# A transformer-like block on one core: the first phase's transfers in program order on one queue

## The chip, the cores and the metric

The kernel runs on one core of a Trainium2 chip. The time is device microseconds of that core for one execution; 2199.59 us is the median of three (2198.95 to 2201.4). One further execution was recorded by the hardware profiler. It took 2197.51 us, and its span, from the first instruction to the last, is 2195.7 us. Engines are named as in the profile: PE multiplies, PEld loads its weights, DVE, ACT and POOL work elementwise, and SP only issues transfers. SPq is SP's queue: it issues in order, and a transfer whose data or target is not ready holds up all that stand behind it.

## The reference

`x` is 8 sequences ("batches" below) of 1024 rows with 512 features. Both branches start from the same layer norm, and their product is added to `x`:

```python
def _L0_attn_ref(x, Wq, Wk, Wv, Wo, Wg, decay_logits, out_scale):
    q = x @ Wq
    gate = softmax(x @ Wg, axis=-1)
    for i in range(3):
        k = x @ Wk[i]
        v = x @ Wv[i]
        w = sigmoid(decay_logits[i]) ** expn * causal     # a later row only
        retrieved = (q @ k.T * w) @ v
        blended = blended + gate[..., i:i + 1] * retrieved
    return blended @ Wo * out_scale

def _L0_ffn_ref(x, lut, gate_idx, up_idx, down_idx):
    h = silu(x @ lut[gate_idx].T) * (x @ lut[up_idx].T)
    return h @ lut[down_idx].T

xn = layernorm(x)
out = x + attn(xn) * silu(ffn(xn))
```

The FFN's weights are given as indices into a table of 16 words, so they have to be looked up before they can be multiplied.

## The kernel before

The program has two phases. **Phase 1** (`phase_1`, up to about 627 us) normalizes and transposes `x`, does the attention, and builds the FFN's weights; it leaves its results in DRAM. **Phase 2** does the FFN and the output. Only phase 1 and the border between the two are touched here.

Phase 1 runs a loop over `b` from 0 to 8, each with eight steps `k`. In loop `b` three generators advance by turns, and so does the building of the weights:

- `project(b)`, called `newer`: for row tile `c = 7 - k` it transposes `x` on PE into PSUM (`pt`), and ACT copies that to `xnT` (L329). Then come `values` (`pv`, then `v`), `features` (`pq`, then `qT` and `kT`) and half a `softmax`, which makes the gates `g` on DVE. The gates go to DRAM as `gTd` (L355) and return, broadcast over the partitions, as `ga` (L359).
- `project(b-1)`, called `ending`: the rest of the previous batch. In steps 0 to 3 DVE makes the sums `ts` (L417) for phase 2, and PE the other half of the features. At the end of the generator, three transfers write `xnT` (L424, L425) and `ts` (L426) to DRAM as `xsd`. In the program this end is reached only when loop `b` has run all its steps.
- `chunks(b-1)`, called `older`: the attention itself, with `pk`, `psc`, `pu` and `po` on PE, `pr` (L468) and `ga` times `qT` (L441) on DVE. ACT copies `po` into `bl` (L489), and after the eighth chunk the whole `bl` is written as `bld` (L503).
- `weights`: for each tile, index loads (`idx`), a tree of table look-ups on DVE (L176 to L200), sums on POOL, and the writes `wgud`, `quadd` and `wdd`. `build_some` advances it by single yields, spread between the other steps.

Buffers that matter: `xnT` has two, so batch `b` writes where batch `b-2` lay. `ts` has one. `x` tiles have four, `idx` and `wgu` two each.

PE, DVE, ACT and POOL keep the order in which the program was traced; `keep_order` links each instruction to the one before it on its engine. SP has that only for its first instructions: `keep_order(tc, seen, (mybir.EngineType.SP,))` is called in `phase_1` ahead of the loop. After these, the framework's scheduler places the transfers on SP's queue.

In the order that it made, the two `xsd<-xnT` of a batch stand in the loop that fills `xnT`, or just behind it, and `xsd<-ts` in the middle of the next loop, where the sums are done; all three come before the `bld` of that next loop.

At the border phase 2 starts with `load_x(0)` (L599), which reads `xsd` of batch 0 into `xs`. Its place in SBUF overlaps buffers of phase 1, so it waits for the last batch's `xsd` writes too. `zs` (L878) are matmuls that keep PE running meanwhile, and `fs` (L631) is the first that needs `xs`.

Of the kernel before, what the change touches and what calls it, by code (L numbers as in the profile page):

```python
# [2 lines left out]

# [7 lines left out]
F32 = mybir.dt.float32  # L11
# [27 lines left out]
def recurrent_block(ctx: ExitStack, tc, x, wq, wk, wv, wo, wg, decay_logits, out_scale, lut, gidx, uidx, didx, out):  # L39
# [51 lines left out]
    def more_weights(wvg_sb, wqk_sb):  # L91
        nc.scalar.dma_start(out=wvg_sb[:, :, NI * D :], in_=wg.rearrange("(c p) d -> p c d", p=P))
        for i in range(NI):
            nc.scalar.dma_start(
                out=wvg_sb[:, :, i * D : (i + 1) * D], in_=wv[i].rearrange("(c p) d -> p c d", p=P)
            )
        yield
        nc.sync.dma_start(out=wqk_sb[:, :, :D], in_=wq.rearrange("(c p) d -> p c d", p=P))
        for i in range(NI):
            nc.sync.dma_start(  # L100
                out=wqk_sb[:, :, (i + 1) * D : (i + 2) * D], in_=wk[i].rearrange("(c p) d -> p c d", p=P)
            )
        nc.sync.dma_start(out=wo_sb, in_=wo)


    seen = {i.name for i in nc.cur_bb.bb.instructions}
# [95 lines left out]

        yield from tree(dst, 3, 0)

    def gate_up_weights(build, pool, pair_pool):

        for o, (s, m) in enumerate(OCH):  # L210
            n = 2 * NV * m
            idx = build.tile([P, NB], I32, name="idx", tag="idx", bufs=2)
            iv = idx[:, :n].rearrange("p (a b) -> p a b", b=m)
            gs, us = (src[:, s : s + m].rearrange("(c p) b -> p c b", p=P) for src in (gidx, uidx))
            nc.sync.dma_start(out=iv[:, 2:6, :], in_=gs)
            nc.sync.dma_start(out=iv[:, 0:2, :], in_=us[:, 0:2, :])
            nc.sync.dma_start(out=iv[:, 6:8, :], in_=us[:, 2:4, :])
            wf = pool.tile([P, 2 * NB], F32, name="wgu", tag="wgu", bufs=2)
            yield from look_up(build, wf[:, :n], idx[:, :n], P, n)
            w = wf[:, : 2 * n].rearrange("p (k two m) -> p k two m", two=2, m=m)  # L220
            a21, a11, a12, a22, s1, s2, s3, s4 = (w[:, k] for k in range(8))
            nc.gpsimd.tensor_tensor(s1, a21, a22, ALU.add)
            nc.gpsimd.tensor_tensor(s2, s1, a11, ALU.subtract)
            yield
            nc.gpsimd.tensor_tensor(s3, a11, a21, ALU.subtract)
            nc.gpsimd.tensor_tensor(s4, a12, s2, ALU.subtract)
            nc.sync.dma_start(out=wgu_d[o], in_=wf[:, 2 * m : 2 * n].rearrange("p (a b) -> p a b", b=m))
            if o < 4 * NQ:
                if o % 2 == 0:
                    upper = w[:, 1:]  # L230
                    continue
                lower = w[:, 1:]
                to = quad_d[o // 4][:, :, o // 2 % 2, :].rearrange("p k (t m) -> p k t m", m=P)
                pair = pair_pool.tile([P, 7, 4, P], F32, name="pair", tag="pair")
                nc.sync.dma_start(out=to[:, :, 0:2, :], in_=upper)
                nc.sync.dma_start(out=to[:, :, 2, :], in_=lower[:, :, 1, :])
                b21, b22, b11, b12 = lower[:, :, 0], lower[:, :, 1], upper[:, :, 0], upper[:, :, 1]
                nc.gpsimd.tensor_tensor(pair[:, :, 0], b21, b22, ALU.add)
                yield
                nc.gpsimd.tensor_tensor(pair[:, :, 1], pair[:, :, 0], b11, ALU.subtract)  # L240
                yield
                nc.gpsimd.tensor_tensor(pair[:, :, 2], b11, b21, ALU.subtract)
                yield
                nc.gpsimd.tensor_tensor(pair[:, :, 3], b12, pair[:, :, 1], ALU.subtract)
                nc.sync.dma_start(out=to[:, :, 3:7, :], in_=pair)
                for _ in range(3):
                    yield

    def down_weights(build, pool):

        s, m = OCH[-1]
        idx = build.tile([P, NB], I32, name="idx", tag="idx", bufs=2)
        nc.sync.dma_start(out=idx[:m, :V], in_=didx[s : s + m, :])
        wf = pool.tile([P, 2 * NB], F32, name="wgu", tag="wgu", bufs=2)
        yield from look_up(build, wf[:m, :V], idx[:m, :V], m, V)
        nc.sync.dma_start(out=wdt_d, in_=wf[:m, :V])
        for j in range(NK):
            idx = build.tile([P, NB], I32, name="idx", tag="idx", bufs=2)
            for a in range(2):
                nc.sync.dma_start(out=idx[:, ts(a, V)], in_=didx[ts(j + a * NK, P), :])  # L260
            t = pool.tile([P, 2 * NB], F32, name="wgu", tag="wgu", bufs=2)
            yield from look_up(build, t[:, : 2 * V], idx, P, 2 * V)
            b11, b12, b21, b22, t1, t2, t4 = (t[:, ts(k, V // 2)] for k in range(7))
            nc.gpsimd.tensor_tensor(t1, b12, b11, ALU.subtract)
            nc.gpsimd.tensor_tensor(t2, b22, t1, ALU.subtract)
            yield
            nc.gpsimd.tensor_tensor(b12, b22, b12, ALU.subtract)
            nc.gpsimd.tensor_tensor(t4, b21, t2, ALU.subtract)
            nc.sync.dma_start(out=wd_d[j], in_=t[:, : 7 * V // 2])


    def warm_up(n):
# [5 lines left out]
    def project(b, pools, sides, kept):  # L278
# [52 lines left out]
        def values(c):  # L331

            pv = p_a.tile([P, NI * D + NI], F32, name=f"pv{b}_{c}", tag="a")
            for v in range(NV):
                nc.tensor.matmul(  # L335
                    pv, lhsT=xnT[:, v, ts(c, P)], rhs=wvg_sb[:, v, :], start=(v == 0), stop=(v == NV - 1)
                )
            nc.scalar.copy(v_sb[:, c, :], pv)

        def softmax(hf):  # L340

            n = NC // NHALF
            logits = gt[:, ts(hf, n), :]
            g = small.tile([P, n, NI], F32, name=f"g{b}_{hf}", tag="g")
            red = small.tile([P, n, 1], F32, name=f"red{b}_{hf}", tag="red")
            nc.vector.tensor_reduce(red, logits, AX.X, ALU.max)
            nc.vector.tensor_tensor(g, logits, red.to_broadcast([P, n, NI]), ALU.subtract)
            nc.scalar.activation(g, g, AF.Exp)
            yield
            sm = small.tile([P, n, 1], F32, name=f"sm{b}_{hf}", tag="sm")  # L350
            nc.vector.tensor_reduce(sm, g, AX.X, ALU.add)
            nc.vector.reciprocal(sm, sm)
            nc.vector.tensor_tensor(g, g, sm.to_broadcast([P, n, NI]), ALU.mult)
            with nc.allow_non_contiguous_dma(reason="1536 words"):
                nc.sync.dma_start(  # L355
                    out=gT_d[b][ts(hf, n * NI), :].rearrange("k p -> p k"), in_=g.rearrange("p c i -> p (c i)")
                )
            gates.append(att.tile([P, n * NI, P], F32, name=f"ga{b}_{hf}", tag="ga"))
            nc.sync.dma_start(out=gates[-1], in_=gT_d[b][ts(hf, n * NI), :].partition_broadcast(P))  # L359

        def features(hf, j):

# [25 lines left out]
        for k in range(NC):  # L388
# [9 lines left out]
                warm_up(5)  # L398
            yield
            if k >= NC // 2:  # L400
                features(1, k - NC // 2)
            half = softmax(1) if k == NC // 2 + lag else iter(())
            next(half, None)
            yield
            next(half, None)
            if k >= lag:
                values(c + lag)
            if lag and k == NC - 1:
                values(0)
            yield  # L410
        ts_ = tp.tile([P, 4, 2, U], F32, name=f"ts{b}", tag="ts")
        b11, b12, b21, b22 = (xnT[:, 2 * r : 2 * r + 2, ts(hf, U)] for r in (0, 1) for hf in (0, 1))
# [10 lines left out]
            yield  # L423
        nc.sync.dma_start(out=xs_d[b][:, 0:4, :], in_=xnT[:, :, :U])  # L424
        nc.sync.dma_start(out=xs_d[b][:, 4:6, :], in_=b22)  # L425
        nc.sync.dma_start(out=xs_d[b][:, 6:14, :], in_=ts_.rearrange("p a b u -> p (a b) u"))  # L426

    def chunks(b, pools, kept):

# [75 lines left out]
    def phase_1():  # L505
        nonlocal small, p_a, p_c, p_r
        with (
# [13 lines left out]
            tc.tile_pool(name="small", bufs=3) as small,  # L521
        ):
            pools = (xp, xnp, tp, att)
            weights = chain(gate_up_weights(build, wgup, pairp), down_weights(build, wgup))
            wvg_sb = wts.tile([P, NV, NI * D + NI], F32, name="wvg_sb", tag="wvg_sb")
            wqk_sb = wts.tile([P, NV, (NI + 1) * D], F32, name="wqk_sb", tag="wqk_sb")

# [11 lines left out]
            next(more)  # L539
            next(newer)  # L540
            next(setup)
            next(more, None)
            keep_order(tc, seen, (mybir.EngineType.SP,))
            for b in range(B + 1):
                following = project(b + 1, pools, (wvg_sb, wqk_sb), kept) if b + 1 < B else iter(())
                older = chunks(b - 1, (chk, blp), kept) if b else iter(())
                for k in range(NC):
                    next(older, None)
                    next(newer, None)
                    next(setup, None)  # L550
                    busy = (b > 0 or k >= NC // 2) and b < B
                    build_some(1 + (0 < b < B))
                    if k < NC // 2:
                        for _ in range(2):
                            next(ending, None)
# [5 lines left out]
                        next(ending, None)  # L561
                    if k >= NC - 2:
                        next(following, None)
                    next(newer, None)
                    next(older, None)
                for g in (older, ending):
# [2 lines left out]
                ending, newer = newer, following  # L569
            for _ in weights:  # L570
                pass

# [385 lines left out]
```

## Time and profile before

| | before |
|---|---|
| median of three runs | 2199.59 us |
| the profiled execution | 2197.51 us |
| its span | 2195.7 us |
| PE busy | 2171.0 us (99%) |
| DVE busy | 1111.9 us (51%) |
| PE's waits that the profile names, all together | 19.1 us |
| granted clock over the span | 0.998 |
| loop 2 / 3 / 4 to 7 / 8 of phase 1 | 75.0 / 74.6 / 74.2 each / 37.1 us |
| first `fs` of phase 2 starts | 627.53 us |

Loops are counted by `b` and measured between their ends: `bld` was issued at 139.55, 215.36, 289.57, 363.79, 438.00, 512.21, 586.42 and 623.54 us. The profile page gives shares of engines first, then the chain of work that ended last, then groups of instructions. The answers of the trace used here are lists of waits by engine (total, times, longest) and timelines (start, length, engine, line, operation; in brackets the idle time before it and what ended it).

### The profile page before, as it was taken

The numbers are of one execution on the slowest core, as the hardware profiler recorded it, in microseconds if no ns is written. First come the engines' busy times: TensorE is split into PE (matmuls) and PEld (weight loads), VectorE is DVE, ScalarE is ACT, GpSimd is POOL, SyncE is SP. The second block draws the span as 40 slices with busy tenths as digits, with TensorE's granted clock in tenths as the row PEclk, the third lists the DMA queues.
The fourth block names the chain that finished last, engine by engine and source line by source line (L and its number), as shares of the span: only waits on it lengthen the run. The fifth ranks groups of instructions, "written<-read, shape, count | busy, mean of one in ns | idle before, by whom it ended". The sixth has DMA issues, their size and how long they took to land.

```text
span 2195.7 us, 25271 instructions
## 1 busy us (share of the span) xinstructions
PE 2171.0 (99%) x9234; PEld 1599.3 (73%) x9234; DVE 1111.9 (51%) x1589; ACT 830.0 (38%) x1795; POOL 912.6 (42%) x800
## 2 busy tenths in 40 slices
PE   8989999999999999999999999999999999999998
PEld 5656666666668778678858876885787678578867
DVE  5866868688635534433533443353344335433533
ACT  3556666666434214312421441243144124313410
POOL 2525454334243454424525441543445153434512
PEclk9999999999999999999999999999999999999999
DMA  5766655534284424334432442343244234234501
GB/s 140 203 160 212 162 163 181 181 125 170 83 327 151 149 99 154 114 115 139 161 122 82 153 130 106 132 155 105 105 154 147 106 116 151 89 132 147 164 24 53
DMA packets 137153, 305.29 MB, mean 139 GB/s; under 512 B 50147, under 2 KB 71910, under 8 KB 136006
## 3 DMA queue, kind: packets, MB, share of 16 engines
q1 hardware_dynamic: 127190, 279.03, 39.1%
q0 software_dynamic: 7728, 23.86, 3.0%
q8 instruction: 73, 1.20, 0.2%
q10 hardware_dynamic: 2112, 0.79, 0.1%
q14 instruction: 50, 0.41, 0.1%
HBM read 225.72 MB, written 77.93 MB: 138 GB/s over the span
## 4 chain that ended last, share of the span: by engine, by line
PE 94%; DMA 3%; DVE 1%; POOL 1%; issue 1%; ACT 1%; ACTq 0%; SPq 0%; POOLq 0%; DVEq 0%
PE s L677 27%; PE ds L821 22%; PE fs L631 9%; PE pq L368 8%; PE pv L335 6%; PE sE L677 4%; PE fsE L631 4%; PE po L488 3%; PE ds L832 2%; PE ps L843 2%; PE psc L466 2%; PE pu L474 1%; PE pt L328 1%; DMA x<-in_x 1%; PE pk L457 1%; DMA xs<-xsd 1%
## 5 line engine op out<-in xcount | busy, mean ns | idle before, releaser
L677 PE MATMUL s<-xs,wq 128*128 128x256 f32 x2688 | 602.9, 380 | 0.0
L677 PEld LDWEIGHTS s<-xs,wq 128*128 128x128 f32 x2688 | 508.7, 190 | 78.4 <-DVE sE L704 2.7
L821 PE MATMUL ds<-wd,s 128*128 128x256 f32 x1280 | 286.7, 379 | 0.0
L821 PEld LDWEIGHTS ds<-wd,s 128*128 128x128 f32 x1280 | 243.2, 190 | 33.0
L368 PE MATMUL pq<-xnT,wqk_sb 128*128 128x512 f32 x512 | 230.3, 592 | 0.0
L821 PE MATMUL ds<-wd,h 128*128 128x256 f32 x960 | 222.9, 379 | 0.0
L821 PEld LDWEIGHTS ds<-wd,h 128*128 128x128 f32 x960 | 182.3, 190 | 52.5 <-issue 27.0
L631 PE MATMUL fs<-xs,wr 128*128 128x512 f32 (+1 forms) x480 | 215.4, 592 | 0.3 <-DMA xs<-xsd 0.3
L733 POOL TENSOR_TENSOR u<-u,e 128x512 f32<-128x512 f32 x64 | 79.9, 1270 | 276.0 <-DVE u L729 276.0
L335 PE MATMUL pv<-wvg_sb,xnT 128*128 128x387 f32 x512 | 179.6, 493 | 7.4 <-ACT xnT L329 7.4
L700 DVE TENSOR_TENSOR s<-s,e 128x512 f32<-128x512 f32 x112 | 78.4, 700 | 187.6 <-ACT s L699 187.6
L631 PEld LDWEIGHTS fs<-xs,wr 128*128 128x128 f32 (+1 forms) x480 | 86.8, 181 | 116.1 <-issue 112.4
L368 PEld LDWEIGHTS pq<-xnT,wqk_sb 128*128 128x128 f32 x512 | 92.3, 190 | 91.8 <-issue 91.8
L846 POOL TENSOR_TENSOR gx<-gx 128x512 f32<-128x512 f32 x63 | 80.3, 1275 | 184.6 <-DVE gx L844 141.1
L335 PEld LDWEIGHTS pv<-wvg_sb,xnT 128*128 128x128 f32 x512 | 93.8, 193 | 63.2 <-ACT xnT L329 7.6
L314 POOL TENSOR_SCALAR rstd<-rstd 128x1 f32<-128x1 f32 x56 | 26.9, 481 | 258.8 <-ACT junk L313 258.2
L615 POOL TENSOR_TENSOR xs<-xs 128x1792 f32<-128x1792 f32 (+1 forms) x38 | 127.9, 3382 | 7.6 <-issue 6.6
L704 DVE TENSOR_TENSOR sE<-s,e 128x512 f32<-128x512 f32 x112 | 78.3, 699 | 85.9 <-PE s L677 85.9
L862 ACT ACTIVATE gx<-ds 128x256 f32<-128x256 f32 x32 | 12.3, 384 | 287.1 <-PE ds L832 287.1
L677 PE MATMUL sE<-xs,wq 128*128 128x256 f32 x448 | 115.0, 379 | 0.0
L695 ACT COPY e<-sE 128x512 f32<-128x512 f32 x112 | 65.6, 586 | 123.7 <-PE sE L677 123.7
L737 POOL TENSOR_TENSOR h<-h,e 128x512 f32<-128x512 f32 x64 | 80.0, 1273 | 57.4 <-issue 46.4
(146 smaller groups left out, 3248.6 us busy)
## 6 DMA issues: line engine op xcount, KB each, us to landing
wq<-quadd SPq DMA_DIRECT2D x112, 896.0 KB, 4.5
xs<-xsd SPq DMA_DIRECT2D x8, 3584.0 KB, 12.1
x<-in_x SPq DMA_DIRECT2D x64, 256.0 KB, 5.2
xsd<-ts SPq DMA_DIRECT2D x8, 2048.0 KB, 7.8
gx<-in_x SPq DMA_DIRECT2D x64, 256.0 KB, 2.9
out<-gx POOLq DMA_DIRECT2D x63, 256.0 KB, 2.3
wr<-wgud SPq DMA_DIRECT2D x16, 896.0 KB, 4.6
ga<-gTd SPq DMA_DIRECT2D x16, 768.0 KB, 5.1
```

Of the source, the lines that this page charges most:

```text
L335: nc.tensor.matmul(pv, lhsT=xnT[:, v, ts(c, P)], rhs=wvg_sb[:, v, :], start=(v == 0), stop=(v == NV - 1))
L368: nc.tensor.matmul(pq, lhsT=wqk_sb[:, v, ts(j, D)], rhs=xnT[:, v, ts(hf, U)], start=(v == 0), stop=(v == NV - 1))
L488: nc.tensor.matmul(po, lhsT=lh, rhs=rh, start=(n == 0), stop=(n == len(prods) - 1))
L615: nc.gpsimd.tensor_tensor(o, x1, x2, ALU.subtract)
L631: nc.tensor.matmul(ps, lhsT=w[:, 2 * W_OF[k] + n, :m], rhs=xs[:, X_OF[k], 2 * n : 2 * n + 2, :], start=start and n == 0, stop=stop and n == 1,
L677: nc.tensor.matmul(self.t[n][:, ts(a, H)], lhsT=self.w[:, a, (0, 1, 6, 2, 3, 4, 5)[i - 1], :], rhs=self.xs[:, X_OF[self.k], D_OF[i], :], s ...
L700: nc.vector.tensor_tensor(self.t[1], self.t[1], self.e, ALU.add)
L704: nc.vector.tensor_tensor(self.t[3], self.t[2], self.e, ALU.add)
L733: nc.gpsimd.tensor_tensor(o[:, n], o[:, n], other[:, n], ALU.add)
L737: nc.gpsimd.tensor_tensor(of_h(half, n), of_h(half, n), two(other[:, n]), ALU.mult)
L821: nc.tensor.matmul(ps, lhsT=lhs[k][:, n, :], rhs=wd_sb[n][:, ts(D_OF[k], H)], start=start and n == 0, stop=stop and n == NK - 1, skip_grou ...
L846: (nc.vector if end else nc.gpsimd).tensor_tensor(g, g, xr, ALU.add)
```

## The change

Every transfer of phase 1 now keeps the place on SP's queue in which the program was traced: `keep_order` for SP is called at the end of `phase_1` and not ahead of the loop. To let a transfer stand later than the line that makes its data, `defer(n, issue)` hands it to a list, and `tick()`, called three times a step, issues what has counted down to zero. Four more edits go with that:

- index loads are issued one tile ahead of the tile that is being looked up, and the first comes one build step later;
- in batch 0, where the values lag one step behind, a second tile of values is done at `k = 4`, and the lag ends there; so the softmax comes at `k = 4` and not at `k = 5`;
- loads of `wqk` and `wo` go into the loop's first steps;
- `gTd` is written 2 ticks after its data, and `ga` read 6 ticks after them; `wgud`, `quadd`, `wdd` and `xsd<-ts` are deferred by 2 to 4 ticks.

The two other `xsd` transfers stay at the end of the generator, where the program had them.

```diff
+    later = []
+    def defer(parts, issue):
+        later.append([parts, issue])
+    def tick():
+        for entry in later:
+            entry[0] -= 1
+        for entry in [e for e in later if e[0] <= 0]:
+            later.remove(entry)
+            entry[1]()
...
-            nc.sync.dma_start(out=wgu_d[o], in_=wf[:, 2 * m : 2 * n].rearrange("p (a b) -> p a b", b=m))
+            wide = wf[:, 2 * m : 2 * n].rearrange("p (a b) -> p a b", b=m)
+            defer(3, lambda: nc.sync.dma_start(out=wgu_d[o], in_=wide))
...
+        jobs = [gate_up(o) for o in range(NO)] + [down_tail()] + [down(j) for j in range(NK)]
+        next(jobs[0])
+        yield
+        for job, following in zip(jobs, jobs[1:] + [iter(())]):
+            next(following, None)
+            yield from job
...
-            nc.sync.dma_start(out=gates[-1], in_=gT_d[b][ts(hf, n * NI), :].partition_broadcast(P))
+            ga = gates[-1]
+            defer(2, write)
+            defer(6, lambda: nc.sync.dma_start(out=ga, in_=there.partition_broadcast(P)))
...
             if k >= NC // 2:
+                if lag and k == NC // 2:
+                    values(c + 1)
+                    lag = 0
                 features(1, k - NC // 2)
-            half = softmax(1) if k == NC // 2 + lag else iter(())
+            half = softmax(1) if k == NC // 2 else iter(())
...
         nc.sync.dma_start(out=xs_d[b][:, 0:4, :], in_=xnT[:, :, :U])
         nc.sync.dma_start(out=xs_d[b][:, 4:6, :], in_=b22)
-        nc.sync.dma_start(out=xs_d[b][:, 6:14, :], in_=ts_.rearrange("p a b u -> p (a b) u"))
+        defer(2, lambda: nc.sync.dma_start(out=xs_d[b][:, 6:14, :], in_=ts_.rearrange("p a b u -> p (a b) u")))
...
-            next(more, None)
-            keep_order(tc, seen, (mybir.EngineType.SP,))
             for b in range(B + 1):
...
                 for k in range(NC):
+                    tick()
                     next(older, None)
...
-                    build_some(1 + (0 < b < B))
+                    build_some((b, k) > (0, 0) and 1 + (0 < b < B))
+                    next(more, None)
+                    tick()
...
                     if k >= NC - 2:
                         next(following, None)
+                    tick()
...
             for _ in weights:
                 pass
+            while later:
+                tick()
+            keep_order(tc, seen, (mybir.EngineType.SP,))
```

On PE, ACT and POOL the built kernel has the same instructions as before, with small moves: in batch 0 the values and features change places for four steps, and a few of POOL's sums stand a place later. On DVE the build steps stand two places later. On SP's queue most transfers have moved.

## The prediction

> **What bounds the kernel now.** I read the page's first part, PE's list of waits, and then timelines at the places that this change touches.
>
> ```profile
> PE 2171.0 (99%) x9234; PEld 1599.3 (73%) x9234; DVE 1111.9 (51%) x1589; ACT 830.0 (38%) x1795; POOL 912.6 (42%) x800
> ...
> PE pv L335 <- ACT xnT L329: 7.4, 1, 7.4
> PE pt L328 <- DVE x L320: 4.8, 4, 2.1
> PE psc L466 <- DVE ga L441: 2.8, 1, 2.8
> ```
>
> PE is the bound, so a transfer order can gain only what PE waits: 19.1 us in all. The clock adds a little. In the windows around the longest wait the granted clock is 0.50 from about 121.5 to 128 us, and the `pv` group of eight matmuls at 123.67 took 5.05 us, where it takes 2.77 elsewhere: one long wait costs another 2.3 us. What the change can lose has no such ceiling, so I looked at what each loop of phase 1 needs when it begins. Loop 3 begins at 215.0:
>
> ```profile
> 214.84 1.22 DVE L417 TENSOR_TENSOR ts<-xnT 128x1024 f32<-128x1024 f32 x1
> 215.06 0.27 ACT L489 COPY bl<-po 128x128 f32<-128x128 f32 x1 [0.85 <-PE po L488]
> ...
> 215.36 0.32 SPq L503 DMA_DIRECT2D bld<-bl  x1
> ...
> 216.16 0.60 ACT L329 COPY xnT<-pt 128x512 f32<-128x512 f32 x1
> ...
> 219.73 2.77 PE L335 MATMUL pv<-wvg_sb,xnT 128*128 128x387 f32 x8
> 219.93 0.56 DVE L468 TENSOR_TENSOR pr<-psc,w_tab 128x384 f32<-128x384 f32 x1 [1.22 <-PE psc L466]
> ...
> 223.01 0.83 PE L488 MATMUL po<-pr,v 128*128 128x128 f32 x6
> ```
>
> See there: DVE overwrites `ts` 0.2 us before the loop begins, ACT overwrites `xnT` 1.2 us after, and both go ahead at once, because both buffers were written out long before. Nothing is idle on PE. `pr` stands behind `ts` on DVE, and `po` at 223.0 needs `pr`.
>
> **The change, part by part.**
>
> *Where `xsd` stands now.* I compared the order of SP's queue in the two built kernels. In the changed one each loop's end reads: `bld`, `xsd<-xnT` (1024 KB), `xsd<-xnT` (512 KB), then, by loop, an `x` tile (256 KB), index loads (512 KB) or a weight tile (896 KB), then `xsd<-ts` (2048 KB). All of these belong to batch b-1, and they stand behind `bld`, which waits for `bl`, the last thing that the loop makes. The built order also shows the waits on the receiving side: the first `xnT` copy of batches 2 to 7 waits for both `xsd<-xnT`, and the first `ts` of batches 1 to 7 for `xsd<-ts`. In loop 3 that is DVE at 214.84 waiting for a transfer that can be issued only after 215.36.
>
> SP's list of waits already has `SPq L503 <- ACT bl L489: 32.6, 8, 7.2`, so SP stands before `bld` today too, with nothing urgent behind it. [...]
>
> *How long the burst takes.* The nearest row is a burst of the same transfers, 896+2048+256+512 = 3712 KB:
>
> ```profile
> 542.11 0.33 SPq L269 DMA_DIRECT2D wdd<-wgu  x1
> 542.53 0.38 SPq L426 DMA_DIRECT2D xsd<-ts  x1
> 543.01 0.85 SPq L297 DMA_DIRECT2D x<-in_x  x1
> 543.96 1.20 SPq L425 DMA_DIRECT2D xsd<-xnT  x1
> ...
> xsd<-ts SPq DMA_DIRECT2D x1, 2048.0 KB, 10.3
> ...
> xsd<-xnT SPq DMA_DIRECT2D x1, 512.0 KB, 10.7
> ```
>
> The last of it landed at 543.96+10.7 = 554.66, 12.55 us after the first issue: 3.38 us per 1000 KB. [...] From `bld` to `xsd<-ts` the new bursts are 4864 KB (loop 2), 5248 (loops 3, 4, 5 and 7), 4352 (loop 6) and 4096 (loop 8): 16.4, 17.7, 14.7 and 13.8 us by the row.
>
> *What PE loses.* After the landing DVE does `ts` 1.22, two short softmax steps 0.33, two build steps 1.6, `ga` 0.55 and `pr` 0.56: 4.3 us. `po` was due 8.0 us after the loop's begin, and `bld` is issued 0.36 after it. So PE waits 0.36 + burst + 4.3 - 8.0 = burst - 3.3: 13.1 in loop 2, 14.4 in each of loops 3, 4, 5 and 7, 11.4 in loop 6; together 82.1. In loop 8 `po` is due 5.25 us after the begin, `bld` goes at 0.5, and there are no build steps (2.65 us of DVE): 11.7. Sum **93.8 us** [...]. The wait for `xnT` lies inside: `bld` and the two writes are 2048 KB, 6.9 us, so `pv` slips by about 3 us, and then `po` waits for the rest. Behind the waiting `ts` stand all of DVE's build steps; nobody else needs them sooner. Behind the waiting `xnT` on ACT stand the next tile's normalization and the copies of `pq` and `pv`, all ready before 225.
>
> *The clock.* Seven waits of over 7 us. By the row each costs 2.3: **16.1 us**. [...]
>
> *After the wait* DVE needs 9.1 to 9.7 us for a step with `ts` and two to three build steps, PE 8.8. Up to three steps a loop may then be paced by DVE: 0 to 2.6 us a loop; I take 0.5, since these steps ran beside PE without a wait before. **3.5 us.**
>
> *The border.*
>
> ```profile
> 614.20 0.60 SPq L599 DMA_DIRECT2D xs<-xsd  x1
> ...
> 623.54 0.32 SPq L503 DMA_DIRECT2D bld<-bl  x1
> ...
> 627.53 2.84 PE L631 MATMUL fs<-xs,wr 128*128 128x512 f32 x6 [0.27 <-DMA xs<-xsd]
> ```
>
> Now `xs` lands just as PE runs out of filler. It must wait for the last `xsd` writes, as its buffer overlies theirs. In the new order these stand behind the last `bld`: bld, 1536 KB and 2048 KB, 4096 KB or 13.8 us, then `xs` with its 13.3 us from before: 623.54+27.1 = 650.6 in place of 627.5, so 23.1, and 2.3 for the clock. **25.4 us** [...]. The last `wdd` write stands there too and delays nothing else.
>
> *What is gained.* In batch 0, index loads no longer stand before an `x` normalization on DVE, and `x_3` is loaded before the big weights: waits of 2.15, 1.88 and 0.31 before `pt`. The softmax one step earlier brings `ga` sooner: 2.84 before `psc` and 0.67 behind it. In loop 1 the 7.43 us wait, with its 2.3 of clock, came from an `x` tile queued behind `quadd<-pair` at 104.32 that took 13.9 us to land; the new order has that tile before the pair. Together 17.6. The next batch's first tile now stands behind that pair and a `gTd`, and `powd` stands before the `wqk` loads, so I take **15** (9 to 19).
>
> Index prefetch, deferred `wgud`, `quadd`, `wdd`: nothing. PE waited for none of them, DVE has 51% to do, and a step in which DVE had to wait for them would cost only what exceeds the cover of some 3 us between `psc` and `po`.
>
> *Sum*, against the profiled execution: 2197.5 + 93.8 + 16.1 + 3.5 + 25.4 - 15 = 2321.3. The median of the runs is 2.1 above that execution: **2323.4 us**, 5.6% slower.
>
> **The rivals.**
>
> - *Only `xnT` counts* (12%): `xsd<-ts` overtakes the rest of its burst, and lands before `pr` is due. [...] Against: the row above, in which `xsd<-ts` took 10.3 us among others. Then six waits of about 3.2 us for `pv`, no cold clock in the loops: 2197.5+19+25.4-15 = 2227, median **2229**.
> - *Faster* (4%): SP reaches `xsd` early enough that both buffers are free at the loop's begin, and only the 15 us of gain show: **2185**. It decides if `xsd<-ts` is issued some 17 us before the loop's end; the built order has it behind `bld`, and I see no way around that.
> - *Knock-on* (12%): `x` tiles 3 and 2 now both stand behind the second `gTd` of a loop, and that one behind the late `ts`. An `x` load at 148.86, issued just after a `gTd`, took 11.1 us. With 5 us more in seven loops: **2358**.
> - *No effect* (2%): the scheduler moves the transfers back. The built order says otherwise.
>
> **How the numbers follow.** Forecast 70%, the rivals as given. [...] To leave no more than 2 in 10 out I go further down, for a mixture with the first rival: 2265 to 2360. 0.2%, or 4.4 us, is about what a measurement of this kernel can tell from no change. Faster 4%, same 2%, slower 94%.
>
> **What would show it.** In PE's list of waits: seven for `pr` of 8 to 12 us before `po`, six of about 3 for `xnT` before `pv`, one of over 20 for `xs` before `fs`, and no 7.4 in loop 1. In DVE's: `ts` waiting for `xsd` about 15 us, seven times. Distances of `bld` on SP's queue near 90 us, not 74. If these distances stay at 74 to 77, the forecast is wrong.

## The result, and the profile after

| | before | after |
|---|---|---|
| median of the compared runs | 2199.30 us (four) | 2308.65 us (four, 2307.3 to 2309.05) |
| the profiled execution, its span | 2197.51, 2195.7 us | 2307.3, 2305.5 us |
| granted clock over the span | 0.998 | 0.977 |
| loops 2 to 7, between issues of `bld` | 75.8, then 74.2 each | 86.9, 89.5, 88.0, 88.3, 87.9, 88.8 us |
| loop 8 | 37.1 us | 48.4 us |
| last `bld` to first `fs` | 4.0 us | 24.1 us |

The changed kernel is slower: the ratio is 1.0494, with a 95% interval of 1.0476 to 1.0512. The forecast was 2323.4 us, in a range of 2265 to 2360. (The table of before gives 75.0 and 74.6 us for loops 2 and 3; the issue times listed under it give 75.8 and 74.2, and these are used here.) Lines moved with the change: `xnT` is now copied at L361, `ts` summed at L454, `pr` made at L505, `po` at L525, `xsd` written at L461 to L463, `bld` at L540.

First the page's busy times, and the lines of the list of waits (engine, line, what it waited for; total, times, longest) that answer to those of before:

```profile
PE 2200.6 (95%) x9234; PEld 1618.4 (70%) x9234; DVE 1117.5 (48%) x1589; ACT 830.6 (36%) x1795; POOL 901.4 (39%) x800
```

```profile
DVE ts L454 <- DMA xsd<-ts: 102.8, 7, 15.8
...
PE po L525 <- DVE pr L505: 44.9, 7, 9.2
...
ACT xnT L361 <- DMA xsd<-xnT: 37.8, 6, 6.7
...
PE fs L673 <- DMA xs<-xsd: 20.3, 1, 20.3
PE pv L367 <- ACT xnT L361: 20.0, 6, 3.7
```

PE has the same 9234 matmuls and was busy 29.6 us longer with them, so part of them ran at half clock (granted clock 0.50 in the windows below). The rest of the loss is in named waits. DVE waits seven times for `xsd<-ts`, and PE seven times for the `pr` that DVE then makes late; ACT waits six times for `xsd<-xnT`, and PE six times for its copy. The 7.4 us wait in loop 1 is gone. Loop 3 shows one whole such chain; it answers to the timeline of before at 215. The columns are start, length, engine, line and operation, and in brackets the idle time ahead and what ended it:

```profile
220.56 0.34 SPq L540 DMA_DIRECT2D bld<-bl  x1
220.94 0.43 SPq L461 DMA_DIRECT2D xsd<-xnT  x1
221.42 0.84 SPq L462 DMA_DIRECT2D xsd<-xnT  x1
224.91 1.07 SPq L463 DMA_DIRECT2D xsd<-ts  x1
227.63 0.59 ACT L361 COPY xnT<-pt 128x512 f32<-128x512 f32 x1 [6.14 <-DMA xsd<-xnT]
228.26 5.53 PE L367 MATMUL pv<-wvg_sb,xnT 128*128 128x387 f32 x8 [3.17 <-ACT xnT L361]
235.30 1.23 DVE L454 TENSOR_TENSOR ts<-xnT 128x1024 f32<-128x1024 f32 x1 [15.15 <-DMA xsd<-ts]
238.64 0.55 DVE L505 TENSOR_TENSOR pr<-psc,w_tab 128x384 f32<-128x384 f32 x1
239.24 1.65 PE L525 MATMUL po<-pr,v 128*128 128x128 f32 x6 [4.58 <-DVE pr L505]
...
251.30 0.83 PE L525 MATMUL po<-pr,v 128*128 128x128 f32 x6
```

`bld` goes first, and SP stood before it eight times in the run, 86.9 us in all and up to 14.0; the three `xsd` follow it, and everything else is a consequence: `xnT` is free at 227.6, `ts` at 235.3, 14.7 us after `bld`. Before, both were free at the loop's begin. `pv` takes 5.53 us in place of 2.77 and `po` 1.65 in place of 0.83, at half clock. The windows of the same loop give the clock itself (stretch, its length, PE busy and matmuls, granted clock, DMA share, GB/s):

```profile
225.10:227.20 2.10, 0.00 (x0) 1.00 1.01 316
227.40:234.00 6.60, 5.74 (x10) 0.50 1.03 435
234.20:237.40 3.20, 0.46 (x5) 1.00 0.01 5
237.60:244.20 6.60, 4.96 (x16) 0.50 0.12 4
244.40:247.00 2.60, 2.60 (x9) 1.00 0.06 4
```

The clock falls to half twice: in the gap before `pv`, and, after it has come back, again in the gap before `po`. What PE loses in the first cold spell is hidden in the wait for `pr`; the half clock after 239.2 is a loss of its own. The border shows the same order once more:

```profile
711.37 0.32 SPq L540 DMA_DIRECT2D bld<-bl  x1
...
722.88 0.59 SPq L641 DMA_DIRECT2D xs<-xsd  x1
...
735.43 1.19 PE L673 MATMUL fs<-xs,wr 128*128 128x512 f32 x1 [20.33 <-DMA xs<-xsd]
```

`xs` is issued 11.5 us after the last `bld`, when the `xsd` writes have landed, and `fs` starts 12.5 us after that. Before, it was issued at 614.20, 9.3 us ahead of `bld`.

One wait is new that the prediction did not have, at the very start:

```profile
13.00 0.38 SPq L167 DMA_DIRECT2D powd<-k_tab  x1
13.43 0.48 SPq L235 DMA_DIRECT2D idx<-in_gidx  x1
...
26.82 0.69 DVE L191 TENSOR_SCALAR bit<-idx 128x1024 uint8<-128x1024 uint8 x1 [13.03 <-DMA idx<-in_uidx]
...
28.11 1.09 PE L360 MATMUL pt<-ident,x 128*128 128x128 f32 x4 [10.47 <-DVE x L352]
```

`powd<-k_tab` writes 384 single words. SP stood 4.2 us before it, until POOL had made `k_tab`. The index loads issued behind it (the last at 14.50) landed 12.3 us later, DVE stood for 13 us at the first look-up, and behind that stood the normalization of `x` that PE needed.

### The profile page after: what moved, and what is told of

Same layout as the page of the kernel before. It is cut to its first block, busy times and chain, and to the rows that moved or that the text cites. A ratio compares the mean times of both kernels' runs of the same rounds, so it can differ in the third digit from the quotient of the medians.

```text
span 2305.5 us, 25243 instructions
## 1 busy us (share of the span) xinstructions
PE 2200.6 (95%) x9234; PEld 1618.4 (70%) x9234; DVE 1117.5 (48%) x1589; ACT 830.6 (36%) x1795; POOL 901.4 (39%) x800
## 4 chain that ended last, share of the span: by engine, by line
PE 91%; DMA 5%; DVE 1%; SPq 1%; issue 1%; POOL 1%; ACT 0%; POOLq 0%; DVEq 0%
PE s L719 25%; PE ds L863 21%; PE fs L673 9%; PE pq L404 9%; PE pv L367 6%; PE sE L719 4%; PE po L525 4%; PE fsE L673 4%; DMA xsd<-ts 3%; PE ds L874 2%; PE ps L885 2%; PE psc L503 2%; PE pu L511 1%; PE pt L360 1%; PE pk L494 1%
## 5 line engine op out<-in xcount | busy, mean ns | idle before, releaser
L673 PE MATMUL fs<-xs,wr 128*128 128x512 f32 (+1 forms) x480 | 217.2, 597 | 20.3 <-DMA xs<-xsd 20.3
L404 PE MATMUL pq<-xnT,wqk_sb 128*128 128x512 f32 x512 | 236.3, 605 | 0.0
L367 PE MATMUL pv<-wvg_sb,xnT 128*128 128x387 f32 x512 | 190.0, 516 | 20.0 <-ACT xnT L361 20.0
L904 ACT ACTIVATE gx<-ds 128x256 f32<-128x256 f32 x32 | 12.3, 384 | 287.4 <-PE ds L874 287.4
L482 POOL TENSOR_TENSOR qb<-ga,q_tab 128x384 f32<-128x384 f32 x56 | 66.2, 1181 | 116.7 <-DVE ga L478 68.5
```

What stands on the lines that cost most here:

```text
L367: nc.tensor.matmul(pv, lhsT=xnT[:, v, ts(c, P)], rhs=wvg_sb[:, v, :], start=(v == 0), stop=(v == NV - 1))
L404: nc.tensor.matmul(pq, lhsT=wqk_sb[:, v, ts(j, D)], rhs=xnT[:, v, ts(hf, U)], start=(v == 0), stop=(v == NV - 1))
L482: nc.gpsimd.tensor_tensor(qb, qa, q_tab, ALU.mult)
L673: nc.tensor.matmul(ps, lhsT=w[:, 2 * W_OF[k] + n, :m], rhs=xs[:, X_OF[k], 2 * n : 2 * n + 2, :], start=start and n == 0, stop=stop and n == 1,
```

## The experiments

The theory: the loss is a matter of order. `bld` waits for the loop's last result, the `xsd` of the batch before stand behind it, and the next writers of `xnT`, `ts` and `xs` wait for these. A first rival is that the moved traffic itself costs the time, wherever the burst stands; a second, that other edits of the change cost some of it. The times of one execution are given where no range stands beside them. The kernel before, on the same chips, had medians of 2197.85 us (eight runs; first eight kernels) and 2200.67 us (nine runs; last four, which are `e9`, `e10`, `e11`, `e12`).

### All three writes where their data are made (e1_both)

```diff
+        nc.sync.dma_start(out=xs_d[b][:, 0:4, :], in_=xnT[:, :, :U])
+        nc.sync.dma_start(out=xs_d[b][:, 4:6, :], in_=b22)
         for k in range(NC // 2):
...
+            if k == NC // 2 - 1:
+                defer(2, lambda: nc.sync.dma_start(out=xs_d[b][:, 6:14, :], in_=ts_.rearrange("p a b u -> p (a b) u")))
...
-        nc.sync.dma_start(out=xs_d[b][:, 0:4, :], in_=xnT[:, :, :U])
-        nc.sync.dma_start(out=xs_d[b][:, 4:6, :], in_=b22)
-        defer(2, lambda: nc.sync.dma_start(out=xs_d[b][:, 6:14, :], in_=ts_.rearrange("p a b u -> p (a b) u")))
```

> The changed kernel with all three writes of a batch's xsd moved to where their data are made: the two of xnT at the begin of the loop after the one that fills it, that of ts two ticks behind the last sum. Nothing else differs. My theory (DVE waits for the ts write and ACT for the xnT write, because both stand behind bld): all seven waits at the loops' begins and the 20 us at the border go, loops last 74 to 75 us again, first fs near 622; only the 6 us stay by which the first two loops are shorter: 2191 us (2186 to 2199). Rival (the fixed order as such costs: x tiles behind gTd, weight writes that block SP): most of the 109 us stays, over 2250.

2190.4 us (2189.68 to 2191.42, five runs): 0.9965 of the kernel before, interval 0.9951 to 0.9979, and 118 us below the changed kernel. Loops 2 to 7 take 74.2 us each (loop 3 takes 75.8) and loop 8 37.1, and no wait for `pr`, `xnT` or `xs` is left. PE's list of waits begins with:

```profile
PE pt L360 <- DVE x L352: 9.7, 1, 9.7
```

In loop 2, for one, the `xnT` writes now leave 3 us after the loop's begin (135.12 and 135.63, where `bld` stands at 132.26), a whole loop ahead of the next writer, and the `ts` write at 160.74, 46 us ahead of the next `bld`. The place of three transfers a batch is the whole loss. What is left is the wait at the start.

### One part at a time (e2_xnT, e3_ts, e9_border)

`e2_xnT` moves only the two `xnT` writes, `e3_ts` only the `ts` write, each with the lines above. `e9_border` is `e1_both` with the writes of the last batch alone left at the generator's end:

```diff
-        nc.sync.dma_start(out=xs_d[b][:, 0:4, :], in_=xnT[:, :, :U])
-        nc.sync.dma_start(out=xs_d[b][:, 4:6, :], in_=b22)
+        late = b == B - 1
+        if not late:
+            nc.sync.dma_start(out=xs_d[b][:, 0:4, :], in_=xnT[:, :, :U])
+            nc.sync.dma_start(out=xs_d[b][:, 4:6, :], in_=b22)
...
-            if k == NC // 2 - 1:
+            if not late and k == NC // 2 - 1:
...
+        if late:
+            nc.sync.dma_start(out=xs_d[b][:, 0:4, :], in_=xnT[:, :, :U])
+            nc.sync.dma_start(out=xs_d[b][:, 4:6, :], in_=b22)
+            defer(2, lambda: nc.sync.dma_start(out=xs_d[b][:, 6:14, :], in_=ts_.rearrange("p a b u -> p (a b) u")))
```

> Only the two writes of xnT are moved to the loop's begin; the write of ts stays behind bld. My theory (the wait for ts is the main one): the waits of pv for xnT go, DVE still waits, for a burst of 3712 KB in place of 5248, so about 12 us; PE waits some 9 us before po, and the clock falls once in place of twice: 2197.5-6+7x11+20 at the border = about 2288. Rival (the wait for xnT is the main one, that for ts would be hidden behind pv): under 2240.

> Only the write of ts is moved, the two of xnT stay behind bld. My theory: DVE doesn't wait any more; six waits of pv for xnT of 3 to 3.7 us stay, each with 2 to 3 us of clock (about 35 us), and some 18 at the border, as bld and 1536 KB are still ahead of xs: about 2243. Rival (xnT is the main wait): over 2275. The two gains of this run and of the one with xnT moved need not add up, since both waits overlap.

> All three xsd writes early for batches 0 to 6, and behind the last bld only for batch 7, as in the changed kernel. My theory (border and loops cost apart): loops as in the kernel with all moved, 20 us of wait before the first fs and 5 us of clock behind it, of which 4 us of filler matmuls are no part: 2190 + 25 = 2215. Rival (xs is late only because the whole phase is late): 2190 to 2195.

They took 2277.4, 2243.2 and 2215.2 us. The lost time by place, each against `e1_both` by distances between `bld` and `fs`:

| late | loops 2 to 8 | border |
|---|---|---|
| `ts` only (`e2_xnT`) | 69.0 | 16.0 |
| `xnT` only (`e3_ts`) | 33.2 | 16.4 |
| both (the changed kernel) | 93.8 | 20.5 |
| both, last batch only (`e9_border`) | none | 21.7 |

PE's waits in `e2_xnT`:

```profile
PE po L525 <- DVE pr L505: 50.5, 7, 8.6
PE fs L673 <- DMA xs<-xsd: 15.8, 1, 15.8
```

and in `e3_ts`, where L674 is `fs`:

```profile
PE pv L367 <- ACT xnT L361: 21.1, 6, 3.7
PE fs L674 <- DMA wdt<-wdtd: 16.2, 1, 16.2
```

Each part alone makes its own wait. With `ts` alone late, DVE waits up to 12.0 us, as expected, but the whole run is some 11 us shorter than expected: 69 us in place of 77 in the loops, where `po` waits 7.2 us each time and not 9, and 16 in place of 20 at the border. `xnT` alone is as expected: 5.5 us a loop, of which 3.5 are the wait and the rest half clock. That is dear for gaps of 3.5 us. The loops' losses do not quite add up, 102 alone and 94 together, as part of the wait for `xnT` lies inside that for `pr`. In `e3_ts` and `e9_border` the list puts the wait before `fs` down to `wdt`, which SP issues about 2.5 us behind `xs`; only the place of the `xsd` writes was changed there.

### The scheduler's order, all else kept (e4_sched)

```diff
+            keep_order(tc, seen, (mybir.EngineType.SP,))
             for b in range(B + 1):
...
-            keep_order(tc, seen, (mybir.EngineType.SP,))
```

> The changed kernel with SP's order fixed only ahead of the loop, as before, so that the scheduler places the later transfers; all other edits stay (deferred issues, indices one tile ahead, values in four slots). My theory: no bld in front of xsd, so near the time of before, 2185 to 2205. Rival (one of the other edits costs): over 2220.

2184.1 us, 0.9 below the range expected. So on balance the other edits cost nothing; without the fixed order they gain 14 us together. The second rival falls.

### The burst just ahead of `bld` (e7_drain)

From the changed kernel, with the `ts` write not deferred, and the ending generator drained before the older one:

```diff
-        defer(2, lambda: nc.sync.dma_start(out=xs_d[b][:, 6:14, :], in_=ts_.rearrange("p a b u -> p (a b) u")))
+        nc.sync.dma_start(out=xs_d[b][:, 6:14, :], in_=ts_.rearrange("p a b u -> p (a b) u"))
...
-                for g in (older, ending):
+                for g in (ending, older):
```

> The changed kernel with one thing turned round: at a loop's end the rest of project is run before the rest of chunks, and the write of ts isn't deferred, so that SP has both xnT writes and the ts write directly ahead of bld, in place of behind it. Sizes and the rest of the order stay. My theory (it is bl's wait at the head of SP's queue that makes the burst late): SP reaches the burst some 8 to 12 us before the loop's end, it lands within 1 to 3 us of the begin, DVE waits little or not and PE not at all; at the border xs starts near its old place: 2188 to 2200. Rival (a burst of this size at this place costs wherever bld stands): over 2230.

2204.4 us, 4 above what was expected. The same bytes leave in the same burst at almost the same place, and 104 of the 118 us are gone. Ahead of loop 3, SP's queue issued the three at 205.38, 205.86 and 206.41 and `bld` at 212.47, a head start of 7.1 us. It differs by loop, and the loops follow it:

| loop | 2 | 3 | 4 | 5 | 6 | 7 | 8 |
|---|---|---|---|---|---|---|---|
| head start of the first `xsd` | 7.7 | 7.1 | 11.5 | 14.2 | 14.1 | 9.2 | 14.0 |
| the loop's length | 79.1 | 78.0 | 74.6 | 74.2 | 74.2 | 75.5 | 37.1 |

DVE still waits four times for `xsd<-ts` (in loops 2, 3, 4 and 7), 21.4 us in all, and `fs` waits 3.1. So the passing of `bld` is most of it, and how far ahead is the rest.

### Traffic that nobody waits for (e8_burst, e10_act)

`e1_both`, and at each loop's end 3584 KB from a constant into memory that nothing reads, on SP's queue (`e8_burst`) or on ACT's (`e10_act`, `nc.scalar`):

```diff
+                if b:
+                    idle = dram.tile([4, P, NV, (NI + 1) * D], F32, name=f"idle{b}", tag=f"idle{b}")
+                    for n in range(3):
+                        nc.sync.dma_start(out=idle[n], in_=wqk_sb)
+                    nc.sync.dma_start(out=idle[3, :, :2], in_=wqk_sb[:, :2])
```

> The kernel with all three xsd writes moved early, and behind each bld a burst of the same 3584 KB that nobody waits for (a constant weight tile written to unused DRAM, so more is written than the reference needs). My theory (only the waits on the buffers cost, not the traffic): 2190 to 2198. Rival (the traffic at the loop's begin delays x tiles, gTd and ga): over 2215. At the border the burst is ahead of fbl and the weights for later, and may cost a few us.

> The kernel with the burst of 3584 KB that nobody waits for, now issued from ACT's queue in place of SP's. It cost 49 us on SP's queue, in waits for ga, x and wr that stand behind it. Theory A (they wait their turn behind the burst in the same queue): on another queue they pass it, and most of the 49 us goes: under 2208. Theory B (the 16 engines share their bandwidth, whichever queue): over 2225.

2239.7 us: my theory missed by over 40, and the rival's side was hit. The first lines of PE's waits, then one of DVE's:

```profile
PE fs L679 <- DMA wr<-wgud: 12.9, 1, 12.9
PE pv L367 <- ACT xnT L361: 11.5, 6, 2.9
...
PE po L526 <- DVE pr L506: 6.1, 1, 6.1
```

```profile
DVE ga L479 <- DMA ga<-gTd: 53.5, 8, 9.6
```

The burst delays other transfers that are needed soon. In loop 3 `gTd` was issued at 222.17, and SP, which holds the read of `ga` until it has landed, could issue that only at 240.97, 18.8 us later; in `e1_both` the same `gTd` landed in 10.9. DVE waits for `ga` 4.7 us in all in `e1_both`, and 9.1 in the changed kernel. Two things keep this from saying that the burst costs 49 us there as well: `e8_burst` adds its bytes to those of `xsd`, where the change only moves them, and in the changed kernel such delays lie beside the longer wait for `ts`. `e7_drain`, which has the same bytes in a burst, loses 14 us with its waits for `ts` and `xs` counted in: the traffic alone costs no more than that there. So the first rival is right that a burst has a price, and wrong on its size.

Was it the one queue, in which the transfers stand behind each other? `e10_act` says no. With the burst on ACT's queue, the `gTd` of loop 3 on SP's queue still took 18.3 us. From 210 to 225 us, a stretch that holds most of the burst of loop 3, the packets of ACT's queue took 41.0% of the time of the 16 DMA engines, and those of SP's queue 39.1%. The whole run took 2255.6 us, worse and not better; but that is not the burst's traffic alone, as here ACT itself is held: its `ks` waited 10.2 us for the burst's own transfers, and 19.3 us is put down to a late `x`.

### The wait at the start (e5_defer, e5_act, e12_best)

`e5_defer` is `e1_both` with the 384 words written behind the first two tiles of indices:

```diff
-        with nc.allow_non_contiguous_dma(reason="384 words, once"):
-            nc.sync.dma_start(out=pow_d[:, P:].rearrange("i s -> s i"), in_=k_tab)
+        def powers():
+            with nc.allow_non_contiguous_dma(reason="384 words, once"):
+                nc.sync.dma_start(out=pow_d[:, P:].rearrange("i s -> s i"), in_=k_tab)
+
+        defer(5, powers)
```

`e5_act` leaves them in their place, and issues them from ACT's queue:

```diff
-            nc.sync.dma_start(out=pow_d[:, P:].rearrange("i s -> s i"), in_=k_tab)
+            nc.scalar.dma_start(out=pow_d[:, P:].rearrange("i s -> s i"), in_=k_tab)
```

> The kernel with all three xsd writes moved early, and the write of k_tab to powd (384 single words) put behind both index tiles, the wqk loads and x_2, in place of ahead of them. My theory (that write is slow in the queue and holds the index loads that DVE stands before): DVE's wait of 12.6 us for idx and PE's of 9.7 go, in part back at x_1, which now stands behind it: 2190 less 5 to 10, 2180 to 2186. Rival (the index loads are late because SP issues them late, at 13.4 us): DVE waits as before, 2189 to 2192.

> The kernel with all three xsd writes moved early, and the write of k_tab issued from ACT's queue, in place of SP's. Theory: on a queue of its own the slow write doesn't stand ahead of the index loads: DVE's wait for idx falls from 12.6 to under 5, PE's from 9.7 to under 3: 2180 to 2186. Rival ([...] the other queue doesn't help): 2189 to 2192.

2178.9 and 2182.2 us. In `e5_defer` PE's list of waits begins with:

```profile
PE po L529 <- POOL qb L486: 1.4, 1, 1.4
PE warm L311 <- POOL nhalf L125: 1.4, 1, 1.4
```

Two shorter ones follow, 3.5 us in all. `fs` starts at 609.05, 10.8 us sooner than in `e1_both` and 18.5 sooner than in the kernel before. In `e5_act` DVE's wait for the indices fell from 12.6 to 0.4 us. The place of the words is the cause, in two ways. The first line is SP's wait in `e1_both`; the others are index loads with their size and the time to landing, in `e1_both` behind the words, in `e5_act` of the second tile, and in `e5_defer` of the second tile:

```profile
SPq L167 <- POOL k_tab L164: 4.2, 1, 4.2
...
idx<-in_gidx SPq DMA_DIRECT2D x1, 256.0 KB, 12.0
...
idx<-in_gidx SPq DMA_DIRECT2D x1, 256.0 KB, 8.7
...
idx<-in_gidx SPq DMA_DIRECT2D x1, 256.0 KB, 5.0
```

First, SP stood before the words until their data were made, so the loads of the first tile left only at 13.42; in `e5_act` and `e5_defer` they left at 8.87. Here the rival of `e5_defer` is right for some 4 of the 12.6 us. Second, behind the words they took 12.0 us to land; ahead of them, 3.2. `e5_act` gains because the loads that DVE needs now leave before the words do. It doesn't show that another queue keeps the words apart: the second tile's load, issued at 14.15 on SP's queue, 1.1 us behind the words on ACT's, took 8.7 us, where it took 5.0 in `e5_defer`.

`e12_best` is `e5_defer` again, in five executions:

> The kernel with xsd early and the powd write deferred, once more, timed in rounds: 2178.9 again, a ratio of 0.990 to 0.993 to the kernel before. If the single look was a lucky one: 2185 or more.

2182.27 us (2179.94 to 2183.08, five runs), 0.9916 of the kernel before with an interval of 0.9902 to 0.9929. It beats both kernels. The single 2178.9 was a favourable one: in the profile of `e12_best`, `fs` starts at 613.19, only 6.6 us sooner than in `e1_both`. So the words cost 7 to 11 us.

### The earlier softmax (e11_lag)

`e5_defer` with the values of batch 0 lagging to the end, and the softmax one step later, as before the change:

```diff
-                if lag and k == NC // 2:
-                    values(c + 1)
-                    lag = 0
...
-            half = softmax(1) if k == NC // 2 else iter(())
+            half = softmax(1) if k == NC // 2 + lag else iter(())
...
+            if lag and k == NC - 1:
+                values(0)
```

> The kernel with xsd early and the powd write deferred (2178.9 us), but with the values of batch 0 one step behind to the end and the softmax at k = 5, as before. Theory (the earlier softmax brings ga in time for loop 1): a wait before psc of 2 to 4 us and 0.7 behind it: 2181 to 2184. Rival (it is worth nothing once the rest is in place): 2178 to 2180.

2190.3 us, 8.0 above `e12_best` on the same chip, more than expected, and not for the reason expected: no wait before `psc` came back. PE waits once 8.7 us for `xnT`, and ahead of that ACT waits 14.6 us for an `x` tile. That tile stands on SP's queue behind a `gTd`, at 37.85 and 37.39 us; in `e12_best` the two leave at 30.57 and 30.12, and PE waits 2.1 us. So in this run the earlier softmax gains less by an earlier `ga` than by sending `gTd`, and the tile behind it, 7 us sooner.

Two other ways to take the waits away, a second `ts` buffer and a third `xnT`, were not tried.

## Why the prediction was right, and where its sizes were off

The mechanism was right at each step that it rested on: `xsd` behind `bld`, DVE waiting about 15 us seven times, PE waiting for `pr` seven times and for `xnT` six times by 3.3 on average, one wait of 20.3 before `fs`, distances of 87 to 90 us, and no 7.4 us wait in loop 1. `e1_both` shows that these transfers are the cause. It also keeps a fixed order on one queue, and is faster than the kernel before (2190.4 us against 2197.85): what costs is this place in the order, and not a fixed order as such. The sum of 2321.3 us for the profiled execution was 14.0 too high. Its terms:

| term | predicted | measured |
|---|---|---|
| slip of the first `po` in loops 2 to 8 | 93.8 | 77.7 |
| clock after it, and pacing by DVE | 16.1 + 3.5 | 16.0 |
| border | 25.4 | 22.0 |
| gain | 15 | 5.9 |
| all together | 123.8 | 109.8 |

Part of the closeness is luck: the costs were 23.1 us too high, and the gain, which was 9.1 too high as well, took some of that back.

- **The slip.** From `bld` to the first `po` it was 7.65 us in loops 2 to 7 and 4.76 in loop 8; now it is 18.73, 18.68, 19.77, 19.67, 18.34, 19.23 and 13.95. Term by term in loop 3, it is 14.74 us from `bld` to `ts` where 17.7 was predicted, 3.94 from there to `po` where 4.3 was, and `po` was due at 7.65, as predicted. The mis-sized term is the burst. I took 3.38 us for 1000 KB from the row at 542 us, so 17.7 for 5248 KB; it took 14.7. Over the seven loops the bursts took 100.8 us in place of 115.7, which is 14.9 of the 16.1 too many. No one rate holds throughout: the 4352 KB of loop 6 took 14.5, as long as the 5248 of loop 3. Why the row of before was dearer, no run shows.
- **The clock.** The size was nearly right, for a reason that was partly wrong. I counted one cold spell a loop, begun by a wait of over 7 us. That spell came, begun by waits of 4.6 to 9.2 us. But PE mostly went cold once before, in the first gap of 3.2 to 3.7 us before `pv`, which the prediction took to be without effect on the clock. What it lost there is hidden, since `po` had to wait for `pr` in any case; that is also why the named waits for `pr` are not 8 to 12. The loss that counts comes after `po`: to the second `po` it took 12.06 us in loop 3, where 9.48 was usual; 1.7 to 3.0 us in each loop, 16.0 in all. `e3_ts` shows what the short gap costs where nothing hides it, 5.5 us for 3.5.
- **Pacing by DVE.** Not seen: the later `po` of loop 3 are 9.5 us apart, as before.
- **The border.** `xsd` landed in 11.5 us, not 13.8, and `xs` took 12.5, not 13.3; 20.1 us, and 1.9 in phase 2's first matmuls, at half clock until 739.3. The same mis-sized rate.
- **The gain.** This step failed, and it was outside its own bounds of 9 to 19. The prediction put it that "`powd` stands before the `wqk` loads". Between the two stand the index loads of the first look-up, on which DVE waits ahead of the `x` normalization. The waits that were to go did go, but one of 10.5 us came in their place. With this removed `fs` is 10.8 us sooner in `e5_defer` and 6.6 in `e12_best`. So, as an estimate, the gain would have been 12.5 to 16.7 without it, near the 17.6 that I had listed.

Of the rivals, the one in which `xsd<-ts` overtakes its burst did not come about; DVE's waits exclude it. The knock-on by late `x` tiles did not reach PE in the changed kernel, but `e8_burst` shows that such delays are real where no longer wait covers them. "Faster" asked for the transfers to stand 17 us ahead of the loop's end: `e1_both` is that kernel, and `e7_drain`, 7 to 14 us ahead, falls between.

## What to carry to other kernels

Here a write-out held its buffer until it had landed: ACT waited up to 6.7 us to overwrite `xnT`, and DVE up to 15.8 for `ts`. So its place on an in-order queue is set by the buffer's next writer. If that one comes at the loop's begin, the write-out should not stand behind a transfer that waits for the loop's last result; where a generator issues it at its end, look at when that end is reached. Before fixing an order, list for each transfer when its own data are made, what stands directly behind it and who waits for that, the small ones first: a row of single words cost 7 to 11 us here. A second queue helped where the first stood waiting for data: the last index load of the first tile left at 9.89 us in `e5_act`, and at 14.50 in `e1_both`. It did not help transfers that move beside single words (8.7 us in place of 5.0) or beside a burst (18.3 in place of 10.9).

## What the runs showed that I had not expected

- Gaps of 3.2 to 3.7 us were enough to halve the clock, though not each time: `pv` behind them took 2.88 us in loop 4, and 4.56 in loops 2 and 7, against 2.77 warm. In loops 2 to 8 of the changed kernel every stretch at half clock lasts 3.41 us, or two or three times that. In loop 3 the clock fell 2.2 us after the end of PE's last matmul, and 1.0 us before the next.
- 3584 KB a loop that nobody waits for cost 49 us over eight loops, in one place by delaying a 6 KB transfer from 10.9 to 18.8 us; from another queue they delayed it as much.
- A transfer of 384 single words cost in two ways: SP stood 4.2 us for its data, and the loads behind it landed in 12.0 us in place of 3.2. From another queue it still held the load issued 1.1 us behind it to 8.7 us in place of 5.0.
